# A graph network's message phase: gate, square and row sums kept in PSUM, node one-hots made by eight one-tile comparisons

## Chip, core and metric

The kernel runs on one NeuronCore of a Trainium2 chip. The metric is the device time of one execution in microseconds (us). The kernel before takes 3602.45 us, the median of three runs (3601.79, 3602.45, 3603.7).

Engines are named as the profile names them: PE is TensorE's matmul, PEld its weight load, DVE is VectorE, ACT is ScalarE, POOL is GpSimd, SP is SyncE, which here only issues DMAs. L1405 is line 1405 of the kernel before.

## The reference, cut to what matters

A graph of 6250 nodes and 206,250 directed edges, sorted by destination, with 64 features a node and 64 an edge, passes four layers. Each is a layer norm with ReLU, then one graph layer, then an addition to `x`. The third graph layer is the one that changes here:

```python
def _L2_gnn_ref(V, E, src, dst, ...):
    V = leaky_relu(V, 0.2)
    Vp = leaky_relu(V @ pAw + pAb, 0.2) @ pBw + pBb
    x = relu(E @ mlp_w1 + mlp_b1)
    x = relu(x @ mlp_w2 + mlp_b2)
    scale = sigmoid(x @ Bw + Bb)
    shift = x @ Cw + Cb
    msg = scale * Vp[src] + shift
    M = power(clip(msg, EPS, None), 2.0)
    ssum = segment_sum(M, dst, num_segments=n)
    ...
    return power(ssum / maximum(cnt, 1.0)[:, None], 0.5)
```

The other three layers multiply the node features by a normed adjacency matrix (the fourth does so three times).

## The kernel before, in words

**The whole.** `fast` builds the adjacency matrix as counts (`A`, one byte each) and multiplies by it with matmuls; layers one, two and four are such products. `general` is another program for inputs on which `fast` finds its own assumptions broken; it is not entered in these runs. Layer three is the message phase, the loop over `slot` at the end of `fast`.

**Tiling of the message phase.** Edges are cut into G = 202 groups of 1024: 128 partitions (P) by J = 8 edges. A tile of one value an edge and feature is therefore 128 x 512. Group g passes a software pipeline, one stage a slot; slot i works on groups i to i - 6:

- `fetched(i)` (L1370): eight indirect DMAs on POOL, one for each of the J columns, gather rows of `Vp_dram` by the source indices in `src_g` into tile `v` (four buffers). `loaded(i + 4)` fetches the edge features through SP.
- `turned_edges(i)`, `layer(i - 1)`, `layer(i - 2)` and `gates_and_shifts(i - 3)`: transposes and matmuls on PE, each evicted by ACT (`evicted`, L1386), up to `p_bc`, which holds gate and shift of a group in two PSUM banks (one buffer).
- `gated(i - 4)` (L1401): ACT writes the sigmoid of the gate half of `p_bc` to the SBUF tile `gate`.
- `clipped(i - 4)`: DVE multiplies `gate` by `v` into `m` (L1405), adds the shift from PSUM (L1406), clips (L1407).
- `squared(i - 4)`: ACT squares `m` twice, into part 0 of the bf16 tile `m3` (L1412) and over `m` itself in fp32 (L1413). The square is then split into three bf16 parts: DVE subtracts part 0 from `m` (L1468), ACT copies the rest to part 1 (L1469), DVE subtracts that into part 2 (L1480).
- `compared_nodes(i - 4)` (L1417): one DVE comparison of 128 x 1024 elements makes the eight one-hot tiles `to`, laid out with the eight j innermost.
- `summed(i - 5)` (L1424): eight matmuls of `to` with `m3` sum the messages by node into `p_s` (a part of one PSUM bank, one buffer).
- `added_to_nodes(i - 6)`: DVE adds the three parts of `p_s` into the SBUF tile `r_s` (L1432) and then `r_s` times an own/other mask into the node sums `H`, one or two instructions (L1437, L1440).

**Work put between.** A list `todo` holds tasks that share the slots: 392 pieces of a check that A is symmetric (`crossed`: three or four transposing matmuls, L1276, then one DVE comparison from PSUM, L1282) and 84 pieces of layer four's first product (`partial`: 21 matmuls, L748, then one DVE addition, L1301). Both take a buffer `p_sum` from a ring of two PSUM banks. `some_of` runs a number of them at two places in each slot, and `read_them` issues the DVE reading of the one before, so that one reading is always pending. Six times in the phase `finished(c)` adds a run of DVE work over a seventh of the nodes (L1339 to L1344 and `normed_and_split`).

**Order.** PE, ACT and DVE execute this phase in the order in which the code issues it (a manual schedule). POOL holds little but the 1616 gathers, in order. A gather into `v` of group i waits until L1405 of group i - 4 has read that buffer. All eight PSUM banks are taken: two for `p_sum`, one each for `p_e`, `p_1`, `p_2` and `p_s`, two for `p_bc`.

Of the kernel before, what the change touches and what calls it, by code (L numbers as in the profile page):

```python
# [8 lines left out]
F32 = mybir.dt.float32  # L9
BF16 = mybir.dt.bfloat16  # L10
FP16 = mybir.dt.float16
I32 = mybir.dt.int32
AF = mybir.ActivationFunctionType
OP = mybir.AluOpType
AX = mybir.AxisListType

P = 128
N = 6250
D = 64
# [6 lines left out]
J = 8  # L26
G = -(-E // (P * J))
# [581 lines left out]
def halves(g):  # L609


    b, q = divmod(window(g), P // QN)
    return [(b, q, P // QN)] + [(b + 1, 0, q)] * (q > 0 and b + 1 < NB)
# [3 lines left out]
def fast(ctx, tc, bad, x, src, dst, edge_attr, W3, b3, W4, b4, w1, b1, w2, b2, Bw, Bb, Cw, Cb,  # L617
         pAw, pAb, pBw, pBb, out):

    nc = tc.nc  # L620
# [135 lines left out]
    with ExitStack() as ph:  # L756

        ipool = ph.enter_context(tc.tile_pool(name="ipool", bufs=1, reuse_waits="tile"))
        with ExitStack() as first:
# [9 lines left out]
                op0=OP.mult)  # L769
# [6 lines left out]
                                           op0=OP.mult, op1=OP.add)  # L776
# [9 lines left out]
        count = ipool.tile([P, 128, GQ], BF16, name="count")  # L786
# [14 lines left out]
        for c0, c1 in ((0, 3), (3, 10), (10, GC)):  # L801
            for c in range(c0, c1):
# [5 lines left out]
                                    op0=OP.mult, op1=OP.max)  # L808
# [21 lines left out]
        with ExitStack() as ps:  # L830
            psum = ps.enter_context(tc.tile_pool(name="ps0", bufs=1, space=PSUM, reuse_waits="tile"))
            p = psum.tile([P, SG, P], F32, name="p_a", bufs=2)
            nc.tensor.transpose(p[:D, 0, :], W3_sb, ident)
            nc.vector.tensor_copy(W3T, p[:D, 0, :])
            p = psum.tile([P, SG, P], F32, name="p_a", bufs=2)
# [34 lines left out]
            for c in range(GC):  # L870
# [6 lines left out]
                                        op0=OP.is_lt, op1=OP.add, accum_out=n)  # L877
                nc.vector.tensor_add(exact_i[:, c:c + 1], begin[:, c:c + 1], n)
            for c in range(GC):
# [6 lines left out]
                                        op0=OP.subtract)  # L886
                nc.scalar.activation(digits[:, 1, :], run[:, :, 1], AF.Copy)
                p = psum.tile([P, 1024], BF16, name="p_dig")
# [6 lines left out]
                if c % 9 == 8 or c == GC - 1:  # L895
                    c0 = c // 9 * 9
                    p = psum.tile([P, 512], F32, name="p_node")
                    for k in range(3):
# [4 lines left out]
                        for i in range(c0, c + 1):  # L903
# [11 lines left out]
                                    op=OP.add)  # L915
            by_col = ipool.tile([GC, P, 2], F32, name="by_col")
            p = psum.tile([P, 512], F32, name="p_node")
# [7 lines left out]
            p = psum.tile([P, 512], F32, name="p_node")  # L925
# [132 lines left out]
    def prepared(psum):  # L1058

        cpool = apart.enter_context(tc.tile_pool(name="cpool", bufs=1, side="right", reuse_waits="tile"))  # L1060
# [35 lines left out]
        for i in range(4):  # L1096
# [5 lines left out]
            for j0 in range(0, J, 4):  # L1102
                p = psum.tile([P, 4, GH], F32, name="p_turn", bufs=2)
# [19 lines left out]
        for g in range(1, G + 1):  # L1123
            if g == G or window(g) != window(g0):
# [4 lines left out]
                                op=OP.subtract)  # L1129
# [6 lines left out]
                                op=OP.add)  # L1136
        yield

        nc.vector.tensor_scalar(dst_g, dst_g, P - 1, None, op0=OP.bitwise_and)
        lane = cpool.tile([P, G, J], BF16, name="lane")  # L1140
        nc.vector.tensor_copy(lane, dst_g)
        own = cpool.tile([P, P // QN, 2], F32, name="own")
        nc.vector.memset(own[:, :, 0], 0.0)
        for q in range(P // QN):
            nc.vector.memset(own[q * QN:(q + 1) * QN, :q + 1, 0], 1.0)
        nc.vector.tensor_scalar(own[:, :, 1], own[:, :, 0], -1.0, 1.0, op0=OP.mult, op1=OP.add)
        count = cpool.tile([P, P, J], BF16, name="count")
        nc.gpsimd.iota(count, pattern=[[1, P], [0, J]], base=0, channel_multiplier=0,
                       allow_small_or_imprecise_dtypes=True)

        before.close()
# [78 lines left out]
    with ExitStack() as ph:  # L1230
        cpool, w1_d, w2_d, b1_c, b2_c, BC, BC_b, ones, src_g, lane, own, count = made.pop()
        mpool = ph.enter_context(tc.tile_pool(name="mpool", bufs=3, reuse_waits="tile"))
        ps_a = ph.enter_context(tc.tile_pool(name="ps_a", bufs=1, space=PSUM, reuse_waits="tile"))
# [124 lines left out]
        BC_AT, M_AT, SUM_AT, ADD_AT = 3, 4, 5, 6  # L1358
        of = [{} for _ in range(G)]
        ends = [e + ADD_AT for e in ends]  # L1360

        def loaded(g):
            of[g]["e"] = mpool.tile([P, J * D], F32, name="e", bufs=6)
            nc.sync.dma_start(of[g]["e"], edge_attr[g * P * J:(g + 1) * P * J, :].rearrange(
                "(p j) f -> p (j f)", j=J))

        def fetched(g):
            v = of[g]["v"] = mpool.tile([P, J, D], F32, name="v", bufs=4)
            for j in range(J):
                nc.gpsimd.indirect_dma_start(  # L1370
                    out=v[:, j, :], out_offset=None, in_=Vp_dram[:, :],
                    in_offset=bass.IndirectOffsetOnAxis(ap=src_g[:, g, j:j + 1], axis=0))

        def turned_edges(g):
            p = of[g]["p_e"] = ps_a.tile([P, 512], F32, name="p_e")
            e = of[g].pop("e")
            for k in range(J // 2):
                nc.tensor.transpose(p[:, k * P:(k + 1) * P], e[:, k * P:(k + 1) * P], ident)  # L1378
# [5 lines left out]
        def evicted(g, p, t, **how):  # L1384
            of[g][t] = mpool.tile([P, 512], F32, name=t)
            nc.scalar.activation(of[g][t], of[g].pop(p), **how)  # L1386
# [10 lines left out]
                                     h2[:, q * P:(q + 1) * P], BC, start=False, stop=(k == 1))  # L1397

        def gated(g):
            gate = of[g]["gate"] = mpool.tile([P, J, D], F32, name="gate")  # L1400
            nc.scalar.activation(gate, of[g]["p_bc"][:, :, 0, :], AF.Sigmoid)  # L1401

        def clipped(g):
            m = of[g]["m"] = mpool.tile([P, J, D], F32, name="m")
            nc.vector.tensor_mul(m, of[g].pop("gate"), of[g].pop("v"))  # L1405
            nc.vector.tensor_add(m, m, of[g].pop("p_bc")[:, :, 1, :])  # L1406
            nc.vector.tensor_scalar_max(m, m, EPS)  # L1407

        def squared(g):
            m = of[g]["m"]  # L1410
            m3 = of[g]["m3"] = mpool.tile([P, J, 3, D], BF16, name="m3")
            nc.scalar.activation(m3[:, :, 0, :], m, AF.Square)  # L1412
            nc.scalar.activation(m, m, AF.Square)  # L1413

        def compared_nodes(g):
            to = of[g]["to"] = mpool.tile([P, P, J], BF16, name="to")
            nc.vector.tensor_tensor(  # L1417
                to, count, lane[:, g, :].unsqueeze(1).to_broadcast([P, P, J]), op=OP.is_equal)

        def summed(g):  # L1420
            p = of[g]["p_s"] = ps_a.tile([P, 512], F32, name="p_s")[:, :3 * D]
            m3, to = of[g].pop("m3"), of[g].pop("to")
            for j in range(J):
                nc.tensor.matmul(p, to[:, :, j], m3[:, j].rearrange("p t f -> p (t f)"),  # L1424
                                 start=(j == 0), stop=(j == J - 1))

        begun = set()

        def added_to_nodes(g):

            r = mpool.tile([P, D], F32, name="r_s")
            nc.vector.tensor_reduce(r, of[g].pop("p_s").rearrange("p (t f) -> p f t", f=D),  # L1432
                                    axis=AX.X, op=OP.add)
            for k, (b, q0, q1) in enumerate(halves(g)):
                part = own[:, q1 if k else q0, k:k + 1]
                if b in begun:
                    nc.vector.scalar_tensor_tensor(H[:, b, :], r, part, H[:, b, :],  # L1437
                                                   op0=OP.mult, op1=OP.add)
                else:
                    nc.vector.tensor_scalar(H[:, b, :], r, part, None, op0=OP.mult)  # L1440
                    begun.add(b)
            return [b // CB for b, _, _ in halves(g) if last[b] == g and b % CB == CB - 1]

        def slot(i):
            def at(later):
                return 0 <= i - later < G

            if i + 4 < G:
                loaded(i + 4)
            if at(3):  # L1450
                evicted(i - 3, "p_2", "h2", func=AF.Relu, bias=b2_c)
            if at(M_AT):
                gated(i - M_AT)
                clipped(i - M_AT)
            if at(0):
                fetched(i)
                turned_edges(i)
            read_them()
            if at(1):
                layer(i - 1, w1_d, "eT", "p_1")  # L1460
            if at(M_AT):
                squared(i - M_AT)
            n = -(-len(todo) // max(min(k for k in ends if k >= i) + 1 - i, 1))
            some_of(n - n // 2)
            if at(M_AT):
                compared_nodes(i - M_AT)
                m, m3 = of[i - M_AT].pop("m"), of[i - M_AT]["m3"]
                nc.vector.tensor_sub(m, m, m3[:, :, 0, :])  # L1468
                nc.scalar.activation(m3[:, :, 1, :], m, AF.Copy)  # L1469
            done = added_to_nodes(i - ADD_AT) if at(ADD_AT) else []  # L1470
            if at(2):
                layer(i - 2, w2_d, "h1", "p_2")
            if at(BC_AT):
                gates_and_shifts(i - BC_AT)
            if at(0):
                evicted(i, "p_e", "eT", func=AF.Copy)
            if at(1):
                evicted(i - 1, "p_1", "h1", func=AF.Relu, bias=b1_c)
            if at(M_AT):
                nc.vector.tensor_sub(m3[:, :, 2, :], m, m3[:, :, 1, :])  # L1480
            read_them()
            some_of(n // 2)
            if at(SUM_AT):
                summed(i - SUM_AT)
            for c in done:
                finished(c)
# [14 lines left out]
        p_m = ps_a.tile([P, 512], F32, name="p_e")  # L1501
# [11 lines left out]
    with ExitStack() as ph:  # L1513
# [5 lines left out]
        for layer in range(3):  # L1519
# [25 lines left out]
            else:  # L1545
                for s in range(CS):
# [3 lines left out]
                    t = whole[:, :, s % 2 * CW:(s % 2 + 1) * CW]  # L1550
                    p = psum.tile([P, 512], F32, name="p_sum", bufs=2)
# [48 lines left out]
```

## Time and profile before

The table is for one profiled execution, which is slower than the timed runs.

| what | value |
|---|---|
| timed, median of three | 3602.45 us |
| the profiled execution's own time | 4099.17 us |
| its span, first to last instruction | 4097.5 us |
| message phase: first and last gather start | 1038.6 and 3593.1 us |
| PE busy in 1038 to 3594 us, at a mean clock of 0.77 | 1778.7 us |
| DVE busy there | 1204.9 us |
| ACT busy there | 857.4 us |
| POOL busy there | 1592.4 us |
| one gather (L1370), least / median / most | 942 / 947 / 1450 ns |
| DVE on 128 x 512, L1405 / L1406 / L1468 / L1480, mean | 694 / 688 / 688 / 689 ns |
| DVE comparison L1417, mean | 686 ns |

How to read it: the span has three stretches. Before 1038.6 us A is built and the first two layers run; after 3593.1 us come the last slots and the rest of layer four. Both are dense on PE. Between them each slot keeps five engines at work in turn, none of them fully. A row of the profile's groups has line, engine, operation, output<-inputs, shapes and count, then busy time, mean ns of one, and the idle time of the engine just before, with what ended most of it. "remote" and "another core or an unknown queue" stand for a wait whose ending the trace does not explain.

### The profile page before, as it was taken

The numbers are of one execution on the slowest core, as the hardware profiler recorded it, in microseconds if no ns is written. First come the engines' busy times: TensorE is split into PE (matmuls) and PEld (weight loads), VectorE is DVE, ScalarE is ACT, GpSimd is POOL, SyncE is SP. The second block draws the span as 40 slices with busy tenths as digits, with TensorE's granted clock in tenths as the row PEclk, the third lists the DMA queues.
The fourth block names the chain that finished last, engine by engine and source line by source line (L and its number), as shares of the span: only waits on it lengthen the run. The fifth ranks groups of instructions, "written<-read, shape, count | busy, mean of one in ns | idle before, by whom it ended". The sixth has DMA issues, their size and how long they took to land.

```text
span 4097.5 us, 59586 instructions
## 1 busy us (share of the span) xinstructions
PE 3166.7 (77%) x24393; PEld 2174.5 (53%) x24393; DVE 1979.9 (48%) x3899; ACT 1255.6 (31%) x2024; POOL 1667.0 (41%) x1889
## 2 busy tenths in 40 slices
PE   1799999999566657776767677766767776699999
PEld 1566679998233324433434333433334443459999
DVE  6899946322244445544445444554444454561111
ACT  1577740000233333333333333333333333320000
POOL 4100010000566656656665656666566566600000
PEclk9799999999677767788777877878777787799999
DMA  3233355653322222222222222222222222136664
GB/s 101 73 84 101 94 169 190 205 181 118 95 75 61 46 53 74 61 80 57 58 63 74 64 64 67 72 59 58 75 56 61 73 65 66 45 113 194 194 203 152
DMA packets 229312, 388.76 MB, mean 95 GB/s; under 512 B 137573, under 2 KB 139743, under 8 KB 228771
## 3 DMA queue, kind: packets, MB, share of 16 engines
q1 hardware_dynamic: 170420, 321.51, 25.1%
q0 software_dynamic: 55104, 60.65, 7.9%
q8 instruction: 193, 3.16, 0.3%
q10 hardware_dynamic: 3504, 2.70, 0.3%
q14 instruction: 91, 0.75, 0.1%
HBM read 340.47 MB, written 44.24 MB: 94 GB/s over the span
## 4 chain that ended last, share of the span: by engine, by line
PE 55%; DVE 15%; another core or an unknown queue 12%; issue 9%; ACT 7%; DMA 1%; POOL 1%; DVEq 0%; ACTq 0%; SPq 0%; POOLq 0%
PE p_acc L1042 18%; PE p_sum L748 11%; PE p_bc L1396 7%; PE p L1382 6%; PE p_a L861 4%; ACT h L1386 2%; PE p_s L1424 2%; DVE m L1405 2%; DVE m L1406 2%; DVE junk L1282 2%; PE p_bc L1392 2%; PE p_e L1378 2%; PE p_sum L1276 1%; DVE m L1407 1%
## 5 line engine op out<-in xcount | busy, mean ns | idle before, releaser
L1370 POOL DMA_INDIRECT v<-Vp_dram,src_g x1616 | 1592.5, 985 | 1307.2 <-issue 786.4
L1042 PE MATMUL p_acc<-U,piece 128*128 128x192 bf16 x9604 | 814.8, 246 | 0.0
L1042 PEld LDWEIGHTS <-piece 128*128 128x128 fp8e4 x9604 | 796.4, 98 | 11.5 <-issue 4.2
L1396 PE MATMUL p_bc<-BC,h 128*128 128x256 f32 x1616 | 575.3, 485 | 22.7 <-issue 21.3
L1282 DVE SCALAR_TENSOR_TENSOR junk<-p_sum,there 128x512 bf16<-128x512 f32 (+1 forms) x392 | 241.8, 617 | 412.4 <-remote 288.6
L1405 DVE TENSOR_TENSOR m<-gate,v 128x512 f32<-128x512 f32 x202 | 140.2, 694 | 617.8 <-ACT gate L1401 426.8
L1396 PEld LDWEIGHTS p_bc<-BC,h 128*128 128x128 f32 x1616 | 335.2, 230 | 177.7 <-issue 142.0
L1276 PE MATMUL p_sum<-ident_b,piece 128*128 128x128 bf16 x1372 | 161.1, 240 | 335.8 <-DVE junk L1282 268.6
L748 PEld LDWEIGHTS <-U 128*64 128x64 bf16 x4116 | 236.9, 113 | 320.6 <-issue 179.6
L1276 PEld LDWEIGHTS <-piece 128*128 128x128 fp8e4 x1372 | 120.3, 108 | 491.4 <-issue 475.3
L748 PE MATMUL p_sum<-piece,U 128*64 128x448 fp8e4 x2058 | 273.9, 385 | 95.0 <-issue 65.5
L865 ACT ACTIVATE strip<-p_a 128x784 fp8e4<-128x784 f32 x392 | 302.0, 820 | 126.2 <-PE p_a L861 110.0
L1382 PE MATMUL p<-h,w_d 128*128 128x512 f32 x404 | 269.1, 749 | 65.9 <-ACT h L1386 56.2
L1386 ACT ACTIVATE h<-p,b_c 128x512 f32<-128x512 f32 x404 | 262.1, 684 | 186.7 <-remote 75.5
L1052 DVE TENSOR_REDUCE zg<-p_acc 128x128 f32<-128x384 f32 x112 | 56.3, 507 | 523.4 <-PE p_acc L1042 522.9
L1469 ACT ACTIVATE m<-m 128x512 bf16<-128x512 f32 x202 | 127.3, 630 | 542.6 <-DVE m L1468 368.9
L1424 PE MATMUL p_s<-m,to 128*128 128x192 bf16 x1616 | 207.4, 279 | 99.6 <-DVE r_s L1432 56.2
L1392 PE MATMUL p_bc<-BC_b,ones 3*128 3x512 bf16 x404 | 182.2, 451 | 114.7 <-DVE m L1406 97.0
L1412 ACT ACTIVATE m<-m 128x512 bf16<-128x512 f32 x202 | 127.2, 630 | 433.9 <-DVE m L1407 319.3
L1382 PE MATMUL p<-eT,w_d 128*128 128x512 f32 x404 | 246.3, 694 | 13.0 <-ACT h L1386 8.0
L1392 PEld LDWEIGHTS <-ones 3*128 3x128 bf16 x404 | 37.5, 93 | 398.7 <-issue 223.3
L748 PE MATMUL p_sum<-strip,U 128*64 128x448 fp8e4 x2058 | 244.6, 360 | 2.5 <-ACT U L711 1.4
(198 smaller groups left out, 3441.3 us busy)
## 6 DMA issues: line engine op xcount, KB each, us to landing
piece<-A SPq DMA_DIRECT2D x249, 784.0 KB
e<-in_edge_attr SPq DMA_DIRECT2D x202, 256.0 KB
A<-strip SPq DMA_DIRECT2D x14, 2744.0 KB
v<-Vp_dram,src_g POOLq DMA_INDIRECT x1616
there<-A SPq DMA_DIRECT2D x28, 784.0 KB
pairs<-pair SPq DMA_DIRECT2D x1, 1616.0 KB
Vp_dram<-v SPq DMA_DIRECT2D x7, 224.0 KB
out<-X SPq DMA_DIRECT2D x6, 224.0 KB
```

Of the source, the lines that this page charges most:

```text
L748: nc.tensor.matmul(p[half * D:(half + 1) * D, :w], U3[:, b, k, :], at_block, start=(i < 2), stop=(i >= 3 * n - 2))
L865: nc.scalar.activation(strips[s][:, :, col:col + 2 * SG].rearrange("p b (j l) -> p b j l", l=2), p[:, :, :2 * NB].rearrange("p j (b l) -> ...
L1042: nc.tensor.matmul(p[d // 2][:, d % 2 * 3 * D:(d % 2 + 1) * 3 * D], t[:, b, d * P:(d + 1) * P], U3[:, k * CB + b, :, :].rearrange("p t f - ...
L1276: nc.tensor.matmul(p[:, a - a0, :], held["here", i, k][:, a, b * P:(b + 1) * P], ident_b, start=True, stop=True)
L1282: nc.vector.scalar_tensor_tensor(junk[:, :(a1 - a0) * P], p[:, :a1 - a0, :].rearrange("p a q -> p (a q)"), 15.5, of_there, op0=OP.min, op1 ...
L1370: nc.gpsimd.indirect_dma_start(out=v[:, j, :], out_offset=None, in_=Vp_dram[:, :], in_offset=bass.IndirectOffsetOnAxis(ap=src_g[:, g, j:j ...
L1382: nc.tensor.matmul(of[g][p], w, of[g].pop(x), start=True, stop=True)
L1386: nc.scalar.activation(of[g][t], of[g].pop(p), **how)
L1392: nc.tensor.matmul(p_bc[:, 4 * b:4 * b + 4].rearrange("p j o f -> p (j o f)"), ones, BC_b, start=True, stop=False)
L1396: nc.tensor.matmul(p_bc[:, 2 * q:2 * q + 2].rearrange("p j o f -> p (j o f)"), h2[:, q * P:(q + 1) * P], BC, start=False, stop=(k == 1))
L1405: nc.vector.tensor_mul(m, of[g].pop("gate"), of[g].pop("v"))
L1424: nc.tensor.matmul(p, to[:, :, j], m3[:, j].rearrange("p t f -> p (t f)"), start=(j == 0), stop=(j == J - 1))
```

## The change

The results of five steps go elsewhere, one step is cut into eight, and one moves within the slot:

- the sigmoid overwrites the gate half of `p_bc` in PSUM; the tile `gate` is gone;
- the fp32 square goes to a new PSUM tile `p_m`, one buffer of the ring `p_sum`, and the two subtractions (L1468, L1480) read it there; L1468 writes it in place;
- the row sums `r_s` go to columns 192 to 255 of `p_s`'s own bank;
- the node one-hots are made by eight comparisons of 128 x 128, each of one `count` row with one fp32 column of `lane` as a per-partition scalar, into `to` with j outermost;
- `squared` is issued after the first `some_of` of its slot, not before it.

```diff
-        lane = cpool.tile([P, G, J], BF16, name="lane")
+        lane = cpool.tile([P, G, J], F32, name="lane")
...
-        count = cpool.tile([P, P, J], BF16, name="count")
-        nc.gpsimd.iota(count, pattern=[[1, P], [0, J]], base=0, channel_multiplier=0,
+        count = cpool.tile([P, P], BF16, name="count")
+        nc.gpsimd.iota(count, pattern=[[1, P]], base=0, channel_multiplier=0,
...
         def gated(g):
-            gate = of[g]["gate"] = mpool.tile([P, J, D], F32, name="gate")
-            nc.scalar.activation(gate, of[g]["p_bc"][:, :, 0, :], AF.Sigmoid)
+            gate = of[g]["p_bc"][:, :, 0, :]
+            nc.scalar.activation(gate, gate, AF.Sigmoid)
 
         def clipped(g):
             m = of[g]["m"] = mpool.tile([P, J, D], F32, name="m")
-            nc.vector.tensor_mul(m, of[g].pop("gate"), of[g].pop("v"))
-            nc.vector.tensor_add(m, m, of[g].pop("p_bc")[:, :, 1, :])
+            p_bc = of[g].pop("p_bc")
+            nc.vector.tensor_mul(m, p_bc[:, :, 0, :], of[g].pop("v"))
+            nc.vector.tensor_add(m, m, p_bc[:, :, 1, :])
             nc.vector.tensor_scalar_max(m, m, EPS)
 
         def squared(g):
-            m = of[g]["m"]
+            m = of[g].pop("m")
             m3 = of[g]["m3"] = mpool.tile([P, J, 3, D], BF16, name="m3")
+            p_m = of[g]["p_m"] = ps_a.tile([P, 512], F32, name="p_sum", bufs=2).rearrange(
+                "p (j f) -> p j f", f=D)
             nc.scalar.activation(m3[:, :, 0, :], m, AF.Square)
-            nc.scalar.activation(m, m, AF.Square)
+            nc.scalar.activation(p_m, m, AF.Square)
 
         def compared_nodes(g):
-            to = of[g]["to"] = mpool.tile([P, P, J], BF16, name="to")
-            nc.vector.tensor_tensor(
-                to, count, lane[:, g, :].unsqueeze(1).to_broadcast([P, P, J]), op=OP.is_equal)
+            to = of[g]["to"] = mpool.tile([P, J, P], BF16, name="to")
+            for j in range(J):
+                nc.vector.tensor_scalar(to[:, j, :], count, lane[:, g, j:j + 1], None,
+                                        op0=OP.is_equal)
 
         def summed(g):
-            p = of[g]["p_s"] = ps_a.tile([P, 512], F32, name="p_s")[:, :3 * D]
+            of[g]["p_s"] = ps_a.tile([P, 512], F32, name="p_s")
+            p = of[g]["p_s"][:, :3 * D]
...
-                nc.tensor.matmul(p, to[:, :, j], m3[:, j].rearrange("p t f -> p (t f)"),
+                nc.tensor.matmul(p, to[:, j, :], m3[:, j].rearrange("p t f -> p (t f)"),
...
-            r = mpool.tile([P, D], F32, name="r_s")
-            nc.vector.tensor_reduce(r, of[g].pop("p_s").rearrange("p (t f) -> p f t", f=D),
+            p = of[g].pop("p_s")
+            r = p[:, 3 * D:4 * D]
+            nc.vector.tensor_reduce(r, p[:, :3 * D].rearrange("p (t f) -> p f t", f=D),
                                     axis=AX.X, op=OP.add)
...
-            if at(M_AT):
-                squared(i - M_AT)
             n = -(-len(todo) // max(min(k for k in ends if k >= i) + 1 - i, 1))
             some_of(n - n // 2)
             if at(M_AT):
+                squared(i - M_AT)
                 compared_nodes(i - M_AT)
-                m, m3 = of[i - M_AT].pop("m"), of[i - M_AT]["m3"]
-                nc.vector.tensor_sub(m, m, m3[:, :, 0, :])
-                nc.scalar.activation(m3[:, :, 1, :], m, AF.Copy)
+                p_m, m3 = of[i - M_AT].pop("p_m"), of[i - M_AT]["m3"]
+                nc.vector.tensor_sub(p_m, p_m, m3[:, :, 0, :])
+                nc.scalar.activation(m3[:, :, 1, :], p_m, AF.Copy)
...
             if at(M_AT):
-                nc.vector.tensor_sub(m3[:, :, 2, :], m, m3[:, :, 1, :])
+                nc.vector.tensor_sub(m3[:, :, 2, :], p_m, m3[:, :, 1, :])
```

## The prediction

> **What bounds the kernel now.** I read the page, then the gathers alone, then the phase's table of waits, then the timeline. The page's chain and its largest group:
>
> ```profile
> PE 55%; DVE 15%; another core or an unknown queue 12%; issue 9%; ACT 7%; DMA 1%; POOL 1%; DVEq 0%; ACTq 0%; SPq 0%; POOLq 0%
> ...
> L1370 POOL DMA_INDIRECT v<-Vp_dram,src_g x1616 | 1592.5, 985 | 1307.2 <-issue 786.4 <-DVE m L1405 492.4 <-DMA v<-Vp_dram,src_g 25.3
> ```
>
> The chain runs over PE, but 12% of it, 11.8% x 4097.5 = 483 us, is waiting that the trace cannot explain: DVE or ACT held for a PE result whose matmul had long ended. The profiled execution is 4099.17 - 3602.45 = 496.7 us above the median. I take these holds to be of the profiled execution alone (assumed; the sizes fit). Without them POOL has no reason to stand still: its 492 us behind L1405 are the slots that such a hold delays. Its own pace, from the timeline:
>
> ```profile
> 1044.99 0.94 POOL L1370 DMA_INDIRECT v<-Vp_dram,src_g  x1 [0.30 <-issue]
> 1046.24 0.95 POOL L1370 DMA_INDIRECT v<-Vp_dram,src_g  x1 [0.31 <-issue]
> ```
>
> One gather every 1.25 us (29 intervals from 1041.24 to 1077.51: 1.2507), eight a group: 10.0 us a slot. The other engines, where nothing holds them:
>
> ```profile
> 1404.46 0.69 DVE L1405 TENSOR_TENSOR m<-gate,v 128x512 f32<-128x512 f32 x1 [0.83 <-ACT gate L1401]
> 1411.47 0.69 DVE L1405 TENSOR_TENSOR m<-gate,v 128x512 f32<-128x512 f32 x1 [0.96 <-ACT h L1386]
> 1418.48 0.69 DVE L1405 TENSOR_TENSOR m<-gate,v 128x512 f32<-128x512 f32 x1 [0.83 <-ACT gate L1401]
> ```
>
> 7.0 us a slot at full PE clock. So the timed runs should be bound by POOL's gathers. Check, by sums: before the first gather 1038.6 less 9.5 of unexplained chain = 1029.1; 1615 x 1.2507 = 2019.9; after the last gather's start 4097.5 - 3593.1 = 504.4, less 20.7, because in the trace the last L1405 came 22.9 us after that start and a gather lands some 2.1 us after its start (semaphore times in the trace; so 2.2): 483.7. With 1.7 outside the span the floor is **3534.4 us**. The timed 3602.45 is 68 above it.
>
> Those 68 us are in the gathers' length. Median 947 ns, mean 985: 1616 gathers hold 64 us over it. Going through the timeline, 233 are over 20 ns long; 225 of them end 0.82 us after a DVE instruction with two SBUF inputs that was running when the gather began (L1417 72, L1480 60, L1468 50, L1405 33, L1343 and L698 five each): such a gather waits for that one to finish.
>
> ```profile
> 1320.12 0.67 DVE L1417 TENSOR_TENSOR to<-count,lane 128x1024 bf16<-128x1024 bf16 x1
> 1320.26 1.36 POOL L1370 DMA_INDIRECT v<-Vp_dram,src_g  x1 [0.30 <-issue]
> ```
>
> L1417 ends at 1320.80, the gather at 1321.62. By line the excess is L1417 28.4, L1405 12.1, L1468 11.3, L1480 7.9, others 4, sum 64 us. Floor plus 64 = 3598, 4 below the median. L1406 and L1282 (one SBUF and one PSUM input) ran at over 300 gathers' starts and lengthened them by 1 to 2 ns on average.
>
> [...] here L1406 (PSUM) takes 688 ns and L1405 (SBUF) 694, so I use no surcharge.
>
> **The change, part by part.**
>
> *Gate in PSUM.* L1405 keeps one SBUF input, `v`: its 12.1 us go. ACT's write to PSUM instead of SBUF: nothing, ACT is busy 857 of 2556 us. `p_bc` is freed by L1406 as before.
>
> *Square in PSUM.* L1468 and L1480 keep one SBUF input: 11.3 + 7.9 = 19.2 us go. Same length.
>
> *Row sums in PSUM.* L1437 and L1440 cost gathers almost nothing before (0.05 us). `p_s` is now held 0.2 to 0.5 us longer, until they are done; the next `summed` stands at the slot's end, behind the tasks: hidden.
>
> *Eight comparisons.* L1417 goes (28.4 us of collisions, 0.60 us from its start to the next one's). The nearest rows are small instructions of L1437 and L1440:
>
> ```profile
> 3598.43 0.28 DVE L1437 SCALAR_TENSOR_TENSOR H<-r_s,own,H 128x64 f32<-128x64 f32 x1
> 3598.63 0.25 DVE L1440 TENSOR_SCALAR H<-r_s,own 128x64 f32<-128x64 f32 x1
> 3598.82 0.69 DVE L1480 TENSOR_TENSOR m<-m,m 128x512 bf16<-128x512 f32 x1
> ```
>
> 0.19 to 0.20 us from start to start: eight are 1.5 us, DVE does 0.9 us more a slot, at 6.0 (1204.9 / 202) so 6.9 of 10.0: hidden. [...] Uncovered it would be 202 x 0.9 = 180 us. [...] they can hold a gather, as L1341, a tensor_scalar over 448 fp32 in SBUF, did once:
>
> ```profile
> 1468.17 0.40 DVE L1341 TENSOR_SCALAR H<-H 128x448 f32<-128x448 f32 x1
> 1468.26 1.13 POOL L1370 DMA_INDIRECT v<-Vp_dram,src_g  x1 [0.30 <-issue]
> ```
>
> [...] L1440, 0.25 us long, cost a gather at most 7 ns. [...] up to 0.9 us if it has to wait for the whole train (1.5 us train, 1.25 us pace: 1.2 hits of 0.75). I take the low end, 1 us in all; a gain is excluded. Weights of `to` now lie contiguous: PEld L1424 may fall from 151 ns towards L1276's 108; off the path.
>
> *The ring.* `p_m` takes one of two `p_sum` buffers from mid-slot until L1480. New wait: the first task of the slot's second half needs the buffer whose DVE reading is issued after L1480. Behind it on PE stand `summed` and the next slot's transposes. In the full-clock slot of 2085.38 that task ran 4.9 us after L1405, the reading ends at 6.1 and with 1.0 more DVE at 7.1: PE waits 2.2 us. From there PE needs 6 us to the end of the next `gates_and_shifts`, whose gate serves the slot after; two slots need 7.1 + 6.1 + 0.7, so 7.0 each, or DVE's own 7.1. At half clock (slot of 1653.73, 10.95 us) PE comes there 10 us after L1405 and doesn't wait. So hidden under 10.0 at full clock. ACT's second square also waits for a task's reading; DVE's eight comparisons cover that.
>
> *squared moved*: ACT has nothing in `some_of`, so its order stays; no DMA and no queue is passed. *lane, count*: the iota (1.9 us, once) shrinks, before the phase.
>
> **Sum.** 64 - 4 (L1343, L698, L1341 stay) = 60 gained; given back: comparisons 1, L1407 meeting a now unbroken stream 3, the last six slots on DVE 3. 3602.45 - 60 + 7 = **3549 us** (-1.5%).
>
> **Rivals.**
>
> *1. POOL stays the bound and loses its collisions* (60%): 3536 to 3565.
>
> *2. The consumers take over part.* With `partial` (84 x 2.2 us = 0.9 a slot) and `finished` (0.3) a slot is 8.5 us at full clock with the new wait, and near 13 at half clock; the mean passes 10.0 when a third of the time is at half clock. For: the phase's mean clock is 0.77 in the trace. Against: that comes of the holds, and three runs within 0.05% look like a fixed pace. At 10.2 a slot, 202 x 0.15 of the 60 is lost: 3580 (3565 to 3595), 20%.
>
> *3. Nothing*: the 68 us are waits for consumers, not collisions: 3602 +- 7, 7%. The fit of 64 to 68 speaks against.
>
> *4. Slower: the train of comparisons shuts POOL out.* Place: a gather starting in the train. Price up to 0.9 us a slot, 182 us; less 60, 3725; at half that 3633. It decides once a slot loses over 60 / 202 = 0.30 us. For: L1341 did hold a gather, and L1407 was itself held 0.2 us by gathers. [...] 13%.
>
> **How the numbers follow.** A measurement here tells 0.2% (7 us) from no change. Faster: 1 and nearly all of 2, 0.79; same 0.08; slower 0.13. Range: from just below the floor, 3531, over cases 1, 2 and 3 to 3610, which leaves out case 4.
>
> **What would show it.** Right: gathers at 945 to 950 ns mean; no gather ending 0.82 us after L1405, L1468 or L1480; comparisons 0.19 apart, DVE at some 6.9 us a slot; PE's waits at L1276 for DVE longer without a later end. Wrong: gathers still at 985 or more (case 4, by the comparisons); POOL's mean short but the time unchanged (3, or 2 if the slots are over 10 us).

## The result, and the profile after

The changed kernel takes 3549.31 us (median of 4 runs, 3548.7 to 3550.7), the kernel before 3602.12 beside it (4 runs, 3599.57 to 3603.7): ratio 0.9855, 95% interval 0.9841 to 0.9869, 1.5% faster. The profiled execution is one of these runs: 3550.7 us, of which the span is 3548.9.

The page's chain by engine, by line, and the gathers:

```profile
PE 39%; POOL 28%; issue 12%; DVE 10%; DMA 8%; ACT 3%; DVEq 0%; POOLq 0%; ACTq 0%; SPq 0%
POOL v L1370 28%; PE p_acc L1042 21%; PE p_sum L748 8%; DMA v<-Vp_dram,src_g 6%; PE p_a L861 4%; PE p_bc L1396 1%; DVE to L1421 1%; DVE m L1406 1%; DVE m L1407 1%; DVE junk L1282 1%; DMA near<-pairs,begin_i 1%; ACT h L1386 1%; DVE p_sum L1473 1%; PE p L1382 1%; DVE lo L852 0%
...
L1370 POOL DMA_INDIRECT v<-Vp_dram,src_g x1616 | 1536.8, 951 | 836.5 <-issue 798.0
```

The 12% of an unknown queue is gone, and POOL's gathers are the largest line of the chain. A gather takes 951 ns on average instead of 985. Behind `issue` lie 344 us ahead of the first gather and the gaps of 0.30 us between gathers, no more: POOL never stands still in the phase. From the timeline, POOL where nothing is in its way, and two slots of the product (L1406 here, L1405 before):

```profile
1534.28 0.94 POOL L1370 DMA_INDIRECT v<-Vp_dram,src_g  x1 [0.30 <-issue]
1535.53 0.94 POOL L1370 DMA_INDIRECT v<-Vp_dram,src_g  x1 [0.30 <-issue]
```

```profile
1529.43 0.69 DVE L1406 TENSOR_TENSOR m<-p_bc,v 128x512 f32<-128x512 f32 x1 [2.80 <-DMA v<-Vp_dram,src_g]
...
1539.64 0.69 DVE L1406 TENSOR_TENSOR m<-p_bc,v 128x512 f32<-128x512 f32 x1 [3.24 <-DMA v<-Vp_dram,src_g]
```

A gather every 1.25 us as before. DVE waits some 3 us in each of these slots until the slot's last gather has landed (150 of the 202 slots, 518.6 us in all); the slots follow each other at POOL's pace, 10 us, not at DVE's.

The comparisons, and the gather that began among them:

```profile
1532.50 1.39 DVE L1421 TENSOR_SCALAR to<-count,lane 128x128 bf16<-128x128 bf16 x8
```

```profile
1532.97 1.01 POOL L1370 DMA_INDIRECT v<-Vp_dram,src_g  x1 [0.30 <-issue]
```

Eight take 1.39 us, 0.163 from start to start. They cost this gather 60 ns, where the single comparison had cost one 0.41 us.

One collision is left, the clip (L1408, 512 fp32 from SBUF to SBUF):

```profile
1471.29 0.43 DVE L1408 TENSOR_SCALAR m<-m 128x512 f32<-128x512 f32 x1
```

```profile
1471.35 1.18 POOL L1370 DMA_INDIRECT v<-Vp_dram,src_g  x1 [0.30 <-issue]
```

The clip ends at 1471.71 and the gather at 1472.53, 0.81 after it (the other gathers that a clip holds: 0.81 to 0.82). It has one SBUF input and holds gathers all the same. In b2 below, where it reads PSUM, it takes 690 ns instead of 427 and holds none.

**The measure used from here on.** The excess of a kernel is the sum, over all gathers at least 20 ns longer than 946 ns, of what is beyond 946. Each such gather is put down to the DVE instruction that ended 0.80 to 0.83 us before the gather did. "Clip" also takes in gathers that ended 0.10 to 0.13 us after a clip which ran in their last part. In the kernel after the excess is 10.9 us: clip 7.8 (38 at the gather's start, 24 in its last part), L698 1.8, comparisons 0.5, the rest small.

### The profile page after: what moved, and what is told of

Same layout as the page of the kernel before. It is cut to its first block, busy times and chain, and to the rows that moved or that the text cites. A ratio compares the mean times of both kernels' runs of the same rounds, so it can differ in the third digit from the quotient of the medians.

```text
span 3548.9 us, 61115 instructions
## 1 busy us (share of the span) xinstructions
PE 2996.9 (84%) x24393; PEld 2097.9 (59%) x24393; DVE 2096.1 (59%) x5313; ACT 1212.9 (34%) x2024; POOL 1608.9 (45%) x1889
## 4 chain that ended last, share of the span: by engine, by line
PE 39%; POOL 28%; issue 12%; DVE 10%; DMA 8%; ACT 3%; DVEq 0%; POOLq 0%; ACTq 0%; SPq 0%
POOL v L1370 28%; PE p_acc L1042 21%; PE p_sum L748 8%; DMA v<-Vp_dram,src_g 6%; PE p_a L861 4%; PE p_bc L1396 1%; DVE to L1421 1%; DVE m L1406 1%; DVE m L1407 1%; DVE junk L1282 1%; DMA near<-pairs,begin_i 1%; ACT h L1386 1%; DVE p_sum L1473 1%; PE p L1382 1%; DVE lo L852 0%
## 5 line engine op out<-in xcount | busy, mean ns | idle before, releaser
L1370 POOL DMA_INDIRECT v<-Vp_dram,src_g x1616 | 1536.8, 951 | 836.5 <-issue 798.0
L1042 PEld LDWEIGHTS <-piece 128*128 128x128 fp8e4 x9604 | 796.4, 98 | 11.3 <-issue 4.2
L1396 PE MATMUL p_bc<-BC,h 128*128 128x256 f32 x1616 | 555.9, 475 | 0.0
L1406 DVE TENSOR_TENSOR m<-p_bc,v 128x512 f32<-128x512 f32 x202 | 139.7, 692 | 622.9 <-DMA v<-Vp_dram,src_g 518.6
L1415 ACT ACTIVATE m<-m 128x512 bf16<-128x512 f32 x202 | 127.2, 630 | 744.6 <-DVE m L1408 737.6
L1276 PE MATMUL p_sum<-ident_b,piece 128*128 128x128 bf16 x1372 | 148.5, 230 | 202.5 <-DVE junk L1282 148.8
L1276 PEld LDWEIGHTS <-piece 128*128 128x128 fp8e4 x1372 | 105.3, 103 | 359.7 <-issue 267.4
L1421 DVE TENSOR_SCALAR to<-count,lane 128x128 bf16<-128x128 bf16 x1616 | 288.4, 278 | 0.0
L1382 PE MATMUL p<-h,w_d 128*128 128x512 f32 x404 | 246.9, 696 | 39.1 <-ACT h L1386 39.1
L748 PE MATMUL p_sum<-piece,U 128*64 128x448 fp8e4 x2058 | 236.0, 371 | 37.4 <-DVE junk L1282 16.4
L1282 DVE SCALAR_TENSOR_TENSOR junk<-p_sum,there 128x512 bf16<-128x512 f32 (+1 forms) x392 | 241.6, 616 | 26.1 <-DMA e<-in_edge_attr 10.6
L852 DVE TENSOR_TENSOR lo<-count,key 128x2048 bf16<-128x2048 bf16 x196 | 239.0, 1220 | 0.0
L861 PE MATMUL p_a<-hd,lo 128*128 128x98 bf16 x3136 | 194.1, 217 | 32.9 <-DVE lo L852 31.6
```

What stands on the lines that cost most here:

```text
L748: nc.tensor.matmul(p[half * D:(half + 1) * D, :w], U3[:, b, k, :], at_block, start=(i < 2), stop=(i >= 3 * n - 2))
L852: nc.vector.tensor_tensor(t, of.unsqueeze(1).to_broadcast(t.shape), key[:, k, at:at + GB].rearrange("p (h j) -> p h j", j=GQ) .unsqueeze(2 ...
L861: nc.tensor.matmul(p[:, j, :2 * NB], lo[:, g // GQ, :, g % GQ], hd[:, g // GQ, :, g % GQ], start=True, stop=True)
L1042: nc.tensor.matmul(p[d // 2][:, d % 2 * 3 * D:(d % 2 + 1) * 3 * D], t[:, b, d * P:(d + 1) * P], U3[:, k * CB + b, :, :].rearrange("p t f - ...
L1276: nc.tensor.matmul(p[:, a - a0, :], held["here", i, k][:, a, b * P:(b + 1) * P], ident_b, start=True, stop=True)
L1282: nc.vector.scalar_tensor_tensor(junk[:, :(a1 - a0) * P], p[:, :a1 - a0, :].rearrange("p a q -> p (a q)"), 15.5, of_there, op0=OP.min, op1 ...
```

## The experiments

Theory A is the prediction's (the first expectations call it Theory 1): each line with two SBUF inputs has collisions of its own, and takes them along when it goes. The first four runs do one part alone on the kernel before, or undo one in the kernel after.

**a1: the eight comparisons alone.** The kernel before with these lines of the change:

```
-        lane = cpool.tile([P, G, J], BF16, name="lane")
+        lane = cpool.tile([P, G, J], F32, name="lane")
-        count = cpool.tile([P, P, J], BF16, name="count")
+        count = cpool.tile([P, P], BF16, name="count")
...
-            nc.vector.tensor_tensor(
-                to, count, lane[:, g, :].unsqueeze(1).to_broadcast([P, P, J]), op=OP.is_equal)
+            for j in range(J):
+                nc.vector.tensor_scalar(to[:, j, :], count, lane[:, g, j:j + 1], None,
+                                        op0=OP.is_equal)
...
```

> The kernel before with the eight one-tile comparisons alone. Theory 1 (a gather waits for a DVE instruction with two SBUF inputs that runs at its start): L1417's share of the collisions goes, 28 us of 3602, so 3574 (3565 to 3583). Rival 2 (the eight short instructions gain by freeing DVE or the weights' reads, not by collisions): no more than 5 us either way. Rival 4 (the train of tensor_scalar shuts POOL out, and the other parts hid it): over 3602.

Measured: 3607.88 us (14 runs) against 3601.22 for the kernel before beside it, ratio 1.0018 (1.0010 to 1.0026). Not faster; slightly slower.

**a2: the gate alone in PSUM.**

```
-            gate = of[g]["gate"] = mpool.tile([P, J, D], F32, name="gate")
-            nc.scalar.activation(gate, of[g]["p_bc"][:, :, 0, :], AF.Sigmoid)
+            gate = of[g]["p_bc"][:, :, 0, :]
+            nc.scalar.activation(gate, gate, AF.Sigmoid)
...
```

> The kernel before with the gate written in place in PSUM alone. Theory 1: the product keeps one SBUF input, its 33 collisions (12 us) go, so 3590 (3583 to 3596). Rival (the gain of the whole change comes of the comparisons and of shorter DVE work): 3602, within 3 us, since the product takes as long with PSUM as with SBUF.

Measured: 3601.36 us against 3601.22, ratio 0.9999 (0.9991 to 1.0008). No change.

**a3: the square alone in PSUM**, in the ring and at its new place.

```
-            nc.scalar.activation(m, m, AF.Square)
+            nc.scalar.activation(p_m, m, AF.Square)
...
-                nc.vector.tensor_sub(m, m, m3[:, :, 0, :])
+                nc.vector.tensor_sub(p_m, p_m, m3[:, :, 0, :])
...
```

> The kernel before with the squared message alone put into a p_sum buffer of PSUM (and squared moved behind the first half of the tasks). Theory 1: the two subtractions keep one SBUF input, 11 + 8 = 19 us of collisions go, so 3583 (3575 to 3592). Rival (the ring's new wait on PE takes it back): 3600 or more.

Measured: 3588.12 us against 3601.22, ratio 0.9963 (0.9949 to 0.9977): 13 us, less than 19. In the second profile of the kernel before (b1 below) the two subtractions have 10.8 us of excess, and in a3 none; the whole excess is 13.3 us less, which is the gain, so the ring's wait takes nothing back.

**a4: the kernel after with the one comparison back** (the diff of a1 the other way round).

> The kernel after with the one 128x1024 comparison in the place of the eight. Theory 1: the collisions of L1417 come back, 28 us if they are as frequent as before, so 3577 (3568 to 3590); gathers that end 0.82 us after it appear again, and no others. Rival 2: within 5 us of 3549. Rival 4: under 3549.

Measured: 3577.57 us against 3601.22, ratio 0.9933 (0.9919 to 0.9947). That is 28 us over the kernel after, as expected.

So the comparison is worth 28 us where it is the last to go and nothing where it is the first. Theory A falls for the single parts, although its sum was right. What took the comparison's place? The same slot in two kernels; first the kernel before (its second profile, b1 below), DVE and POOL:

```profile
1705.21 0.69 DVE L1417 TENSOR_TENSOR to<-count,lane 128x1024 bf16<-128x1024 bf16 x1
1705.82 0.69 DVE L1468 TENSOR_TENSOR m<-m,m 128x512 f32<-128x512 f32 x1
...
1707.20 0.69 DVE L1480 TENSOR_TENSOR m<-m,m 128x512 bf16<-128x512 f32 x1
```

```profile
1705.32 1.39 POOL L1370 DMA_INDIRECT v<-Vp_dram,src_g  x1 [0.30 <-issue]
1707.02 0.94 POOL L1370 DMA_INDIRECT v<-Vp_dram,src_g  x1 [0.30 <-issue]
```

The comparison holds a gather until 1705.89 + 0.82. The next starts 0.30 later, at 1707.02, when the first subtraction (L1468) is over and the second (L1480) has not begun: neither costs anything. In a1:

```profile
1704.53 1.39 DVE L1418 TENSOR_SCALAR to<-count,lane 128x128 bf16<-128x128 bf16 x8
1705.83 0.69 DVE L1469 TENSOR_TENSOR m<-m,m 128x512 f32<-128x512 f32 x1
...
1707.22 0.68 DVE L1481 TENSOR_TENSOR m<-m,m 128x512 bf16<-128x512 f32 x1
```

```profile
1704.64 0.96 POOL L1370 DMA_INDIRECT v<-Vp_dram,src_g  x1 [0.30 <-issue]
1705.90 1.43 POOL L1370 DMA_INDIRECT v<-Vp_dram,src_g  x1 [0.30 <-issue]
1707.64 1.08 POOL L1370 DMA_INDIRECT v<-Vp_dram,src_g  x1 [0.30 <-issue]
```

The comparisons let the gather of 1704.64 pass, so the next one meets the first subtraction (1.43 us), is held to 0.82 after its end, and so sends the one after that into the second subtraction (1.08 us). All 55 gathers that L1469 held in a1 were followed by one that L1481 held, for 0.14 us on average.

Two things differ between these slots: the hold, and the place of the subtractions. L1468 starts 0.61 us after the one comparison; its twin in a1 starts 1.30 us after the first of the eight, about one interval of POOL's beat (1.25). It is the place that counts. Had the gather of 1705.32 not been held and DVE's lines stayed where they are, the next would have started at 1706.57, after the end of L1468 at 1706.51. Reckoned so over b1's trace (a gather every 1.249 us, held when it starts more than 0.13 us before a line's end), 61 of the 63 gathers that the comparison held would have been followed by four that meet neither subtraction. And in a1, 53 of the 55 gathers that L1469 held came next after one that had begun in the first 0.56 us of the eight, where the single comparison would have held it. The eight comparisons hand these gathers on because they take 0.7 us longer. This is reckoned from the traces; no run removes the hold and leaves the subtractions in their place.

For the gate's product, which takes 0.69 us before and after, it is **theory B**. A held gather sets POOL's beat anew: the next one starts 0.82 + 0.30 = 1.12 us after the end of the line that held it. DVE's lines keep their order, so whatever runs in that time is sheltered, and what runs at 1.12 us is hit. Removing a line gives its gathers to those that it sheltered. By the same reckoning each of the 76 gathers that the product held in b1 would have led to a collision with a later line (41 with the clip, 20 with the first subtraction, 12 with the comparison, 3 with the second subtraction), for 17.3 of its 20.7 us. In a2 the product holds none, the clip and the two subtractions rise from under 1, 4.2 and 6.6 us to 5.1, 16.4 and 10.3, and the sum stays near 60. The reckoning by hand in the expectations is this rule, replayed with DVE's recorded distances against the beat of 1.25 us.

**b1: the kernel before once more.** No edit.

> The kernel before itself, for a second profile. The step of the prediction that is tested: the 483 us of unexplained holds belong to the one profiled execution. Then this profile has a span near 3600, no share for an unknown queue, POOL in the chain, and the gathers hold some 60 us over 946 ns each, so that the span less this excess is 3538, as in the four kernels that have run. Rival: the holds are of the kernel, and come again.

Measured: 3598.72 us, one run, with this page:

```profile
PE 37%; POOL 34%; issue 14%; DMA 8%; DVE 6%; ACT 2%; DVEq 0%; POOLq 0%; ACTq 0%; SPq 0%
...
L1370 POOL DMA_INDIRECT v<-Vp_dram,src_g x1616 | 1588.6, 983 | 836.3 <-issue 804.0
```

No unknown queue, and POOL, with 1% of the chain in the first profile, has 34%: the 483 us of holds belonged to the one execution. Span 3597.1, excess 61.8, difference 3535.4.

**b2: the clip reads PSUM.** The kernel after with

```
-            nc.vector.tensor_add(m, m, p_bc[:, :, 1, :])
-            nc.vector.tensor_scalar_max(m, m, EPS)
+            nc.vector.tensor_add(p_bc[:, :, 1, :], m, p_bc[:, :, 1, :])
+            nc.vector.tensor_scalar_max(m, p_bc[:, :, 1, :], EPS)
```

> The kernel after, with the sum of gate product and shift written in place in PSUM and the clip reading it there, so that the clip is no SBUF-to-SBUF tensor_scalar. Theory: the 38 gathers that the clip holds in the kernel after (5.9 us) go, 3543 (3541 to 3547), and no gather ends 0.82 us after the clip. Rival (what is left is not the clip's doing, or goes over to the comparisons): within 2 us of 3549.

Measured: 3544.06 us (3540.16 to 3544.76) against 3599.77, ratio 0.9843 (0.9829 to 0.9856). Its group of gathers:

```profile
L1370 POOL DMA_INDIRECT v<-Vp_dram,src_g x1616 | 1530.7, 947 | 836.2 <-issue 791.1
```

The clip is longer, 690 ns instead of 484, and holds no gather any more. The excess is 4.0, 6.9 less than in the kernel after, and the time some 5 us less. The two ratios' intervals overlap; the trace carries this reading more than the times do. It is the fastest version that fetches every row.

**b3: gate and comparisons without the square.** The diffs of a1 and a2 on the kernel before. Three theories give three numbers.

> The kernel before with the gate in PSUM and the eight comparisons, without the square. Theory A (the record's sum: each line has its own collisions): 3602 - 28 - 12 = 3562. Theory B (a held gather sets POOL's beat anew against DVE's order, so a line that is freed leaves collisions to the next ones; beat and offsets put together by hand give 44 us of excess from the two subtractions alone): 3538 + 44 = 3582 (3572 to 3592). Theory C (what the single edits gave, added): 3602 + 6 - 0 = 3608.

Measured: 3599.9 us against 3599.77, ratio 1.0000 (0.9991 to 1.0008). A's 3562 is 38 us too low, and B's range ends 8 us short; C is nearest, but says nothing of a cause. B was right on where the time goes: the two subtractions have 46.6 us of excess where 44 was reckoned. It had left out the clip (8.1 us) and the rest (5), which the gate's removal uncovers.

**b4: the comparison 0.32 us later.** The kernel of a4 with, ahead of the comparison,

```
+            for _ in range(2):
+                late = mpool.tile([P, P], BF16, name="late", bufs=1)
+                nc.vector.tensor_scalar(late, count[:, :P // J, :].rearrange("p a j -> p (a j)"), 1.0,
+                                        None, op0=OP.is_equal)
```

> The kernel after with the one 128x1024 comparison (3577.6), and two 128x128 DVE instructions without use ahead of it, which put it 0.32 us later and add DVE work; the collisions' own number and length are unchanged if they belong to the line. Theory A: 3577 again, or a little more if the two hold gathers too. Theory B (the place of the comparison in POOL's beat decides): shifted by 0.2 to 0.4 us the same reckoning gives 17 to 19 us of excess in place of 37, so 3558 (3550 to 3568).

Measured: 3573.86 us, ratio 0.9932 (0.9918 to 0.9946), against 0.9933 for a4: unchanged, as A forecast, and 6 us above B's range. The comparison's excess is 25.6 us, after 30.0. B's shift in the beat was wrong in size here; what rules A out are b3 and c1.

**c1 and c2: the first subtraction's second SBUF input, without and with the comparison ahead of it.** In the kernels after and a4:

```
...
-            nc.scalar.activation(p_m, m, AF.Square)
+            nc.scalar.activation(m, m, AF.Square)
...
-                nc.vector.tensor_sub(p_m, p_m, m3[:, :, 0, :])
+                nc.vector.tensor_sub(p_m, of[i - M_AT].pop("m"), m3[:, :, 0, :])
```

> The kernel after, with the square that the first subtraction reads back in SBUF (its result stays in PSUM), so that one line with two SBUF inputs is left. In the kernel before this line had 4 us of excess in the second profile, 11 in the first. Theory A (each line has its own collisions): 3549 + 4 to 11, so 3553 to 3560. Theory B (there it was sheltered by the comparison ahead of it; alone it is met at a chance place of POOL's beat): an instruction of 0.69 us holds a gather for its remaining time less 0.126 us (0.82 + rest against 0.946), which at an even spread over 1.25 us is 0.127 us a slot, 26 us in all; put together by hand from the offsets of the kernel after, 38. So 3575 to 3587.

> The kernel after with the one comparison and the square of the first subtraction back. Theory A: the comparison alone gave 3577.6; the subtraction adds to it what it adds to the kernel after. Theory B (shelter): it adds clearly less than there, some 5 to 24 us where the reckoning by hand gives 24 beside the comparison and 36 to 38 without it; 3583 to 3602.

Measured: c1 3590.78 us, ratio 0.9967 (0.9955 to 0.9979); c2 3590.29 us, ratio 0.9966 (0.9954 to 0.9979); the kernel before took 3601.33 beside them. The same line costs 41 us alone (3590.8 - 3549.3) and 13 beside the comparison (3590.3 - 3577.6): theory A, which wants the same in both, is out. In the profile of c1 the line has 44.5 us of excess, in c2's 13.4, with 23.8 for the comparison. Alone it is well above the 26 of an even spread, and the time is 4 us above B's range: its place in the beat is no chance one. Shelter is the lesser part of the difference between 41 and 13. Of the 78 gathers that the comparison held in c2 only 14 would otherwise have led to a collision with the subtraction, for 1.7 us by the reckoning above. What differs more is again the place: at the median the subtraction starts 0.83 us after the one comparison in c2 and 1.30 us after the first of the eight in c1, where 97 of the 125 gathers that it held came next after one that had begun in the first 0.56 us of the eight.

**c4: the gate back in SBUF in the kernel after** (the diff of a2 the other way round).

> The kernel after with the gate back in SBUF: of the lines with two SBUF inputs the product alone is left. Theory A: 12 us more, 3561. Theory B: one unsheltered instruction of 0.69 us, 26 us by the even spread and 23 to 28 by the reckoning; the clip behind it is then sheltered and its 6 us go: 3549 + 26 - 6 = 3569 (3563 to 3577).

Measured: 3563.59 us, ratio 0.9891 (0.9876 to 0.9906), 14 us over the kernel after. Both A's 3561 and B's 3563 to 3577 are near it; the parts tell them apart. The product has 20.0 us of excess, and the clip fell from 7.8 to 0.6. Why, from this timeline:

```profile
1089.61 0.69 DVE L1405 TENSOR_TENSOR m<-gate,v 128x512 f32<-128x512 f32 x1 [5.58 <-DMA v<-Vp_dram,src_g]
1090.41 0.69 DVE L1406 TENSOR_TENSOR m<-m,p_bc 128x512 f32<-128x512 f32 x1
1091.13 0.43 DVE L1407 TENSOR_SCALAR m<-m 128x512 f32<-128x512 f32 x1
```

```profile
1089.73 1.39 POOL L1370 DMA_INDIRECT v<-Vp_dram,src_g  x1 [0.30 <-issue]
1091.43 0.95 POOL L1370 DMA_INDIRECT v<-Vp_dram,src_g  x1 [0.30 <-issue]
```

The product holds the first gather. The next starts in the clip's last 0.13 us, and 0.13 + 0.82 is the 0.95 that a gather takes anyway.

**c3: seven gathers a slot.** The kernel after with

```
+            nc.vector.memset(v[:, J - 1, :], 0.0)
-            for j in range(J):
+            for j in range(J - 1):
```

> The kernel after with seven gathers a slot; the eighth block of each tile of fetched rows is set to zero by DVE, so one message in eight is computed from zeros. Theory (POOL's beat is the bound): 202 x 1.25 = 252 us less, 3297, as long as a slot of 8.75 us is enough for the other engines. Rival 2 of the record (the consumers are close behind: 8.5 us a slot at full clock, near 13 at half): over 3340, and gathers that wait for DVE.

Measured: 3294.03 us (3292.48 to 3294.18), 255 us less than the kernel after, 1.26 for each of the 202 gathers left out. The waits of POOL in this phase:

```profile
POOL v L1371 <- issue: 715.5, 1219, 344.3
POOL v L1371 <- DMA v<-Vp_dram,src_g: 34.4, 113, 0.3
POOL v L1371 <- DVE junk L1282: 7.6, 25, 0.3
```

The columns are total, number and longest; apart from the one wait of 344.3 ahead of the phase none is over 0.3, POOL's own gap. Even at 1773.4 / 202 = 8.78 us a slot POOL waits for nobody.

**The profiles together**, in us, without the first one of the kernel before and without c3, which does less work. "Floor" is the span less the excess.

| kernel | two SBUF inputs left | span | excess | product | comparison | subtraction 1 | subtraction 2 | clip | floor |
|---|---|---|---|---|---|---|---|---|---|
| before (b1) | all four | 3597.1 | 61.8 | 20.7 | 26.3 | 4.2 | 6.6 | under 1 | 3535.4 |
| a1 | product, both subtractions | 3600.5 | 61.0 | 19.2 | 0.5 | 23.8 | 12.8 | 0.4 | 3539.5 |
| a2 | comparison, both subtractions | 3597.2 | 59.9 | 0 | 24.2 | 16.4 | 10.3 | 5.1 | 3537.3 |
| b3 | both subtractions | 3598.5 | 59.6 | 0 | 0.4 | 31.0 | 15.6 | 8.1 | 3539.0 |
| a3 | product, comparison | 3587.0 | 48.5 | 18.7 | 25.3 | 0 | 0 | 0.6 | 3538.5 |
| a4 | comparison | 3576.0 | 38.7 | 0 | 30.0 | 0 | 0 | 6.4 | 3537.3 |
| b4 | comparison, later | 3572.0 | 33.8 | 0 | 25.6 | 0 | 0 | 5.4 | 3538.2 |
| c1 | subtraction 1 | 3590.0 | 52.7 | 0 | 0.5 | 44.5 | 0 | 5.4 | 3537.3 |
| c2 | comparison, subtraction 1 | 3581.5 | 45.9 | 0 | 23.8 | 13.4 | 0 | 6.1 | 3535.6 |
| c4 | product | 3562.3 | 23.6 | 20.0 | 0.4 | 0 | 0 | 0.6 | 3538.7 |
| after | none | 3548.9 | 10.9 | 0 | 0.5 | 0 | 0 | 7.8 | 3538.0 |
| b2 | none | 3543.0 | 4.0 | 0 | 0.8 | 0 | 0 | 0 | 3539.0 |

Read the last column first. The spans differ by 57 us, the floors by 4: held gathers are the difference, to within those 4 us. Then read subtraction 1 downward: 4 us with product and comparison ahead of it, 24 behind the eight comparisons, 16 without the product, 31 with both changes, 44 in c1.

## Why the prediction was right, and which of its steps were not

**What bounds the kernel** was right. The holds were of one execution (b1), POOL's gathers set the phase (c3), and the gain is the gathers' lost waiting: 61.8 - 10.9 = 51 us of excess, against 52.8 in the medians.

**The sum of 60, its parts.** The prediction took 12.1 for the gate, 19.2 for the square and 28.4 for the comparisons, as if each could be had by itself. Done first, they gave 0 (a2), 13 (a3) and -7 us (a1). Done last, onto the two others, they gave 14 (c4 to after), 51 (b3 to after, row sums included) and 28 us (a4 to after). The step that failed is the attribution "by line": a held gather belongs to the line that it met, but without the product it would have met one of the lines behind it, and with eight comparisons in the place of one it meets the subtraction that they push back. The sum held all the same, because the change removes every such line of the slot but the clip, and then it does not matter which of them a gather would have met. That it met 3549.31 to less than 1 us is luck: with the sizes found since, b1's 61.8 less 3.8 for the lines that stay, and 0.5, 7.6 and 1.7 given back, the same sum gives 3554. Two of the three parts alone (b3) would have been forecast at 3562 by this working, and took 3600.

**The terms given back.** Comparisons 1 us, an estimate of the author's that no trace had shown: 0.5 measured. L1407 (now L1408) 3 us: 7.8 measured, since the product that had sheltered the clip (0.6 in a3 and c4, which keep it) no longer does; the prediction named the unbroken stream as the reason and was short in size. L1343, L698 and the like, 4: about 2.6. The end, 3: the part from the last gather's start is 485.4 us, 1.7 over the floor's 483.7.

**The floor** of 3534.4 was 5 low: 3538.0 and 1.8 outside the span. Of 9.5 us of holds taken off ahead of the phase, too many were: the first gather starts at 1035.5, not 1029.1. The pace without excess is (2028.0 - 10.9) / 1615 = 1.2490, not 1.2507, 2.8 less; the end takes 1.7 more. The prediction noted 4 us between floor plus excess and the median; for the kernel before the floor was 2.6 low (b1: 3535.4 and 1.6 outside the span), which is part of them.

**DVE and the ring.** Comparisons 0.19 apart and 6.9 us of DVE a slot were forecast; 0.163 and 1337.65 / 202 = 6.6 came. What the prediction left at nothing is that this longer train moves the subtractions in POOL's beat. The weight loads of the one-hots fell from 150 ns to 107, as forecast, off the path. The ring's new wait is there: PE waits at L1276 for L1485, 51.1 us for matmuls and 84.1 for weight loads, on top of 148.8 for L1282 (178 in the same stretch of b1). POOL waits for none of it. The row sums were not tried alone; the floors of a1 to a3 and b3, which lack them, are those of the others.

**The rivals.** Consumers as a second bound (2): out, since a slot of 8.78 us still leaves POOL unhindered. The mean granted clock was 1.00 in the prediction's slots of 7.0 us and 0.50 in its slot of 10.95; over the phase it was 0.77 in the first profile, 0.85 in b1, without the holds, and 0.88 in the kernel after. Waits for consumers instead of collisions (3): out, by the floors. The train that shuts POOL out (4): out; 13 gathers ended 0.81 to 0.82 us after one of the comparisons, but they lost 0.5 us together, not up to 0.9 a slot.

**What stays open.** a1 is 6.7 us above the kernel before in the times, but its profiled run, 3602.26, was the lowest of its 14. Against b1 it has 0.8 us less excess and a floor 4.1 higher, 2.2 of it after the last gather's start; where the rest lies isn't seen. c2's profiled run, 3583.2, was likewise the lowest of six. How much of a1 and of c1 against c2 is place and how much shelter was reckoned, not run. The rule of 1.12 us tells who is sheltered, but its replay missed sizes: 38 for 44.5 in c1, 24 for 13.4 in c2, 18 for 25.6 in b4.

## What to carry to other kernels

When one engine runs a steady beat (here a gather every 1.25 us) and others block it, an excess counted by culprit says what all of them cost together, not what removing one would give: here a held gather set the beat anew, the next one starting 1.12 us after the end of the line that held it, and so the culprit sheltered what ran in that time. A cure that takes longer than the culprit, like the eight comparisons (1.39 us for 0.69), also moves what follows it into the beat. Remove all of them, or count which remaining line stands where the beat will fall. Before giving up on an edit that gains nothing alone, as two of these three do, try it last instead of first.

## What had not been expected of the hardware

A gather that began under the product or one of the two subtractions lost only what remained of that line beyond 0.126 us (0.946 - 0.82): in the first profile of the kernel before 27 began in the last 0.126 us of one, and none of them took over 0.948 us. The clip of 512 fp32 between SBUF tiles also delayed gathers that were in their last part: they ended about 0.1 us after the clip (24 in the kernel after, 1.9 us together). And the clip, 427 ns when nothing is in its way (135 of the 202 in the kernel after took 420 to 429), took 690 from PSUM in b2; the slower instruction made the faster kernel.
